# Row maxima of the first layer: one transfer per group into the query stack in place of four

## The chip, the cores and the metric

The kernel runs on one core of one Trainium2 chip. A core has five engines that work side by side, each on its own list of instructions in order: TensorE (PE: matmuls, with the loading of weights, PEld, counted apart), VectorE (DVE), ScalarE (ACT), GpSimd (POOL) and SyncE (SP). Transfers run on sixteen DMA engines; here SP and ACT issue them, and the issuing instruction stands in the queue of that engine. The metric is the device time in microseconds (us). Before the change the median of three runs is 1673.33 us (1674.31, 1663.47, 1673.33).

## What is computed

Two layers of cross attention, one after the other, over x of shape (16, 256, 320) with a context of shape (16, 256, 512); 20 heads of 16. In the first layer the first 77 context rows are text and the other 179 are image tokens:

```
logits   = q_h @ k_text.T * scale              ; probs = softmax(logits)         # per head
scores   = q_h @ k_ip.T  * scale
text_probs = softmax(q @ k_text.T * scale)      # all heads together
sem      = (text_probs @ text) @ ip.T * scale
ip_probs = softmax(scores + 0.5 * sem) * mask
out      = (probs @ v_text + ip_probs @ v_ip) @ Wout + bout + x
```

Each row of each head has two softmaxes, over text and over image tokens, so there are two maxima per row and head to be subtracted before the exponential. The second layer has 252 text rows and 4 image tokens, and is not touched by the change.

## The kernel before

**Tiling.** Everything is kept transposed where matmuls want it. A batch (of 16) has five *groups* of four heads, so each layer has 80 groups; the main loop has one *slot* per group (`slot0` for the first layer, `slot1` for the second), and beside the groups' work a list of tasks with due times fills the slots with projections, the semantic path, outputs and weights (`fill`). TensorE's order of work is as recorded (it is pinned); that of ACT, DVE, POOL and SP is put together when the program is built, by a scheduler that works through its own estimate of the times, within the dependencies and within a few orders that the code asks for (`queued`, `anchor`).

**A group of the first layer.** The *stacks* Q (`qs`) and K (`ks`) are tiles of 128 partitions by four heads by 256 columns, four of each in rotation. SP loads them (line 82, `stacks0`): 48 rows of query and key parts from DRAM (`qs<-qd`, `ks<-kd`), and 77 rows of the semantic path (`qs<-tph`, `ks<-M`). Rows 125 and 126 of K hold a constant indicator of text and image columns, loaded once (`ks<-mt`); rows 125 and 126 of Q are to hold the maxima: row 125 the maximum over text, row 126 that over image tokens, each for four heads and 256 queries.

The steps around the change, with the lines of the profile:

- `score0(k, t)`: four matmuls (L649) make the scores S of half t of group k. Two reductions on DVE take the maxima over the first 77 columns (L650) and over the other 179 (L651) into `mn`.
- `maxima0(k)`: two matmuls with the identity (L657) turn `mn` into eight rows of 256; ACT copies them to `mt` (L659; there is one such buffer); transfers (L661) bring them to rows 125 and 126 of Q, one per head, from the two rows of `mt` that belong to it. They are issued on ACT's queue, but for groups 0 and 1, whose maxima are issued on SP ahead of the loop (`begin`).
- `turned0(k, t)`: four matmuls (L673) of the whole stacks, 127 rows, make the scores with the maxima subtracted, transposed (T, two banks of PSUM); two exponentials on ACT (L676) make P, and POOL multiplies with the semantic factors (L679). For t = 1 the exponentials stay behind the last of the next group's issues (`queued(exp, issues[k + 1])`).
- `attend0(k)`: 24 matmuls of P with the values (L709), then `settle0` on DVE and POOL (L720 to L729).

Slot k holds, in this order, `maxima0(k + 1)`, `score0(k + 2, 0)`, `turned0(k, 0)`, other work, `attend0(k - 1)`, `score0(k + 2, 1)`, `turned0(k, 1)`, the loads of group k + 4, and other work. So a group's maxima leave about one slot before T needs them.

**Semaphores of transfers.** In the built program eight semaphores serve the transfers of both queues, handed out in turn in the scheduler's order; each issue also waits for the transfer eight before it, which had the same semaphore.

Of the kernel before, what the change touches and what calls it, by code (L numbers as in the profile page):

```python
# [9 lines left out]
FR = mybir.dt.float32r  # L10
AF = mybir.ActivationFunctionType
ALU = mybir.AluOpType
AX = mybir.AxisListType
# [10 lines left out]
T0 = 77  # L24
# [7 lines left out]
KS0 = 127  # L32
KS1 = 50
XROW = 48
# [14 lines left out]
def xattn2(  # L49
# [27 lines left out]
    nc = tc.nc  # L77
    f = lambda ap: ap.bitcast(F32)
    mm = nc.tensor.matmul
# [9 lines left out]
    def bank(tag="X"):  # L89
        return ps.tile([128, 512], F32, tag=tag, name=tag, bufs=BANKS[tag])  # L90

    def scores():

        return ps.tile([128, 1024], F32, tag="S", name="S", bufs=1).rearrange("p (h t) -> p h t", h=4)
# [4 lines left out]
    def buf(tag, shape, dtype=F32, bufs=1, name=None):  # L99
        if tag in ("wB", "wD", "vr", "raw"):  # L100
            return sb.tile(shape, dtype, tag=tag, name=name or tag, bufs=bufs)
        size = 1
        for d in shape[1:]:
            size *= d
        if tag not in slots:
            slots[tag] = [0, dtype] + [const_tile([128, max(size, words.get(tag, 0))], f"{tag}_{i}", dtype) for i in range(bufs)]
        n, kind, *ring = slots[tag]
        assert kind == dtype and len(ring) == bufs, tag
        slots[tag][0] += 1
        t = ring[n % bufs][: shape[0], :size]  # L110
        names = "abcd"[: len(shape) - 1]
        if len(names) > 1:
            t = t.rearrange(f"p ({' '.join(names)}) -> p {' '.join(names)}", **dict(zip(names, shape[1:])))
        return t

    def const_tile(shape, tag, dtype=F32):
        return const.tile(shape, dtype, tag=tag, name=tag)
# [7 lines left out]
    ident_r = const_tile([128, 128], "ident_r", FR)  # L125
# [15 lines left out]
    def anchor(inst):  # L141
        anchors[inst.ins.engine] = inst
        return inst
# [496 lines left out]
    maxes, issues = {}, {}  # L640

    def score0(k, t):
        Q, K = QK[k]
        if t == 0:
            maxes[k] = buf("mn", [128, 2, 4, 2], FR, bufs=2)
        mn = maxes[k]
        sp = scores()
        for h in range(4):
            mm(sp[:, h], Q[: XROW + T0, h, t * 128 : (t + 1) * 128], K[: XROW + T0, h], start=True, stop=True)  # L649
        nc.vector.tensor_reduce(mn[:, t, :, 0], sp[:, :, :T0], axis=AX.X, op=ALU.max)  # L650
        anchor(nc.vector.tensor_reduce(mn[:, t, :, 1], sp[:, :, T0:], axis=AX.X, op=ALU.max))  # L651

    def maxima0(k, queue=nc.scalar):
        Q, mn = QK[k][0], maxes[k]
        mp = bank()
        for t in range(2):
            mm(mp[:8, t * 128 : (t + 1) * 128], mn[:, t].rearrange("p h a -> p (h a)"), ident_r, start=True, stop=True)  # L657
        mt = buf("mt", [8, S], FR)
        nc.scalar.copy(mt, mp[:8, :S])  # L659
        for h in range(4):  # L660
            issues[k] = queue.dma_start(f(Q[XROW + T0 : KS0, h]), f(mt[2 * h : 2 * h + 2]))  # L661

    def turned0(k, t):

# [355 lines left out]
    for c in range(B // 2):  # L1020
        n, k = 10 * c, [("k0", c)] if c else []
# [34 lines left out]
    def ahead(k, t):  # L1056
        if k < NS:
            score0(k, t)
        else:
            both1(k - 2, t)  # L1060
# [5 lines left out]
    def begin():  # L1066
# [15 lines left out]
        stacks0(2)  # L1082
        parts(k0)
        score0(0, 0)
        parts(v1)
        score0(0, 1)
        get("m0t", 1)
        maxima0(0, nc.sync)
        parts(v1)
        get(*v1)  # L1090
# [3 lines left out]
        score0(1, 1)  # L1094
        parts(("s0", 1))
        maxima0(1, nc.sync)
        parts(("k0", 1))
        resid0.append(load(xT_d[0], "xc"))
# [97 lines left out]
```

## Time and profile before

| | us |
|---|---|
| runs | 1674.31, 1663.47, 1673.33; median 1673.33 |
| profiled execution, span from first to last instruction | 1663.4 |
| TensorE busy | 1533.5 (92%) |
| DVE busy | 1317.2 (79%) |
| POOL busy | 1202.2 (72%) |
| ACT busy (issuing not counted) | 877.7 (53%) |
| last issue of the first layer's maxima | 746.6 |
| granted TensorE clock, mean | 0.974 |

The page gives no time of the profiled execution but its span; the lowest of the runs is 0.07 us above it. A row of the profile names the engine, the line of the kernel, the operation and out<-in by the program's names. "Idle before <- X" says how long the engine stood idle and what ended that. The engine names with a q (ACTq, SPq) are the engines' queues: time in them is spent issuing or waiting, and is not counted as busy. The chain of waits follows back from the last instruction to what released it, step by step.

### The profile page before, as it was taken

What the parts mean: (1) busy time and instruction counts of PE and PEld (TensorE: products, weight loads), DVE (VectorE), ACT (ScalarE), POOL (GpSimd) and SP (SyncE); (2) the same over time, 40 slices, a digit from 0 to 9 for tenths busy, and PEclk for the clock granted to TensorE, in tenths of its full rate; (3) what the DMA queues carried; (4) which work ended last, traced back from release to release, by engine and by line L of the source; (5) the groups of instructions that cost most, each with busy time, mean ns of one, the idle gap of its engine ahead of it and who ended that gap; (6) DMA issues with size and microseconds to landing.
All of it is one profiled execution on the core that took longest, in us unless ns stands there. A gap on an engine that the chain in (4) does not pass through costs nothing.

```text
span 1663.4 us, 35253 instructions
## 1 busy us (share of the span) xinstructions
PE 1533.5 (92%) x12666; PEld 1222.9 (74%) x12666; DVE 1317.2 (79%) x2484; ACT 877.7 (53%) x1865; POOL 1202.2 (72%) x1194
## 2 busy tenths in 40 slices
PE   7789999999999898789999999999999999999996
PEld 6677888787888786677677777777777777777754
DVE  5367676777776677867889889889888998899885
ACT  5344444444444445435656555655565556556563
POOL 3458787878787767767778777867876777777784
PEclk9899999999999899899999999999999999999998
DMA  7867777777776676655424342434243324332301
GB/s 219 218 196 212 200 215 197 211 202 213 198 220 194 192 203 185 159 178 153 147 66 129 106 128 90 133 106 129 85 131 113 120 89 131 117 105 82 115 17 43
DMA packets 247739, 247.43 MB, mean 149 GB/s; under 512 B 31050, under 2 KB 231468, under 8 KB 247564
## 3 DMA queue, kind: packets, MB, share of 16 engines
q1 hardware_dynamic: 245356, 243.87, 49.7%
q8 instruction: 101, 1.65, 0.4%
q10 hardware_dynamic: 2208, 1.30, 0.3%
q14 instruction: 74, 0.61, 0.1%
HBM read 121.21 MB, written 88.18 MB: 126 GB/s over the span
## 4 chain that ended last, share of the span: by engine, by line
PE 55%; DVE 18%; DMA 10%; POOL 4%; SPq 4%; issue 3%; ACT 3%; ACTq 0%; DVEq 0%; POOLq 0%
PE X L205 14%; PE X L814 12%; PE X L522 8%; PE P L709 5%; DMA qs<-qd 4%; SPq L82 4%; PE S L649 3%; DVE mn L781 3%; DVE wt L818 3%; PE T L673 3%; PE P L826 3%; PE T L775 2%; DVE wt L816 2%; PE P L828 2%; DVE ho L512 2%
## 5 line engine op out<-in xcount | busy, mean ns | idle before, releaser
L679 POOL TENSOR_TENSOR P<-P,rs 128x512 f32<-128x512 f32 x320 | 412.2, 1309 | 169.3 <-ACT P L676 169.0
L805 POOL TENSOR_TENSOR wt<-P,ctb 128x512 f32<-128x512 f32 x320 | 451.0, 1424 | 76.0 <-ACT ctb L804 75.6
L814 PE MATMUL X<-ctb,gm 128*128 128x512 f32 x1120 | 329.3, 412 | 2.5 <-DVE wt L816 2.5
L676 ACT ACTIVATE P<-T 128x512 f32<-128x512 f32 x320 | 176.1, 595 | 233.8 <-PE T L673 128.3
L786 ACT ACTIVATE P<-T 128x512 f32<-128x512 f32 x320 | 173.9, 597 | 138.8 <-PE T L775 137.4
L816 DVE TENSOR_TENSOR wt<-X,wt 128x512 f32<-128x512 f32 x320 | 215.3, 678 | 17.4 <-PE X L814 16.9
L804 ACT ACTIVATE ctb<-P 128x512 fp32r<-128x512 f32 x320 | 195.3, 632 | 61.5 <-PE X L814 60.8
L814 PEld LDWEIGHTS X<-ctb,gm 128*128 128x128 f32 x1120 | 189.6, 188 | 48.6 <-DVE wt L816 5.2
L781 DVE TENSOR_REDUCE mn<-S 128x4 fp32r<-128x1008 f32 x160 | 191.1, 1194 | 0.6 <-PE S L780 0.6
L651 DVE TENSOR_REDUCE mn<-S 128x4 fp32r<-128x716 f32 x160 | 142.6, 891 | 0.0
L673 PE MATMUL T<-qs,ks 127*128 127x256 f32 x640 | 112.5, 296 | 22.9 <-DVE tmp L726 9.9
L709 PE MATMUL P<-P,vr 128*32 128x256 f32 x1920 | 129.3, 405 | 0.0
L649 PE MATMUL S<-ks,qs 125*128 125x256 f32 x640 | 117.7, 308 | 11.7 <-DMA ks<-kd 4.6
L649 PEld LDWEIGHTS S<-ks,qs 125*128 125x128 f32 x640 | 88.7, 195 | 48.6 <-issue 38.4
L522 PE MATMUL X<-ho,wF 128*128 128x256 f32 x768 | 112.4, 289 | 6.7 <-DVE ho L512 2.9
L522 PE MATMUL X<-hq,wE 128*128 128x256 f32 x768 | 111.9, 289 | 5.8 <-ACT hq L511 3.1
L818 POOL TENSOR_TENSOR wt<-wt 128x512 f32<-128x512 f32 x80 | 103.3, 1292 | 14.8 <-DVE wt L816 14.7
L673 PEld LDWEIGHTS T<-qs,ks 127*128 127x128 f32 x640 | 93.0, 198 | 28.0 <-DVE tmp L726 11.9
L522 PEld LDWEIGHTS X<-ho,wF 128*128 128x128 f32 x768 | 103.0, 194 | 12.5 <-DVE ho L512 4.6
L522 PEld LDWEIGHTS X<-hq,wE 128*128 128x128 f32 x768 | 102.7, 194 | 11.4 <-POOL hq L512 5.2
L650 DVE TENSOR_REDUCE mn<-S 128x4 fp32r<-128x308 f32 x160 | 74.9, 468 | 44.1 <-PE S L649 43.6
L818 DVE TENSOR_TENSOR wt<-wt 128x512 f32<-128x512 f32 x80 | 106.1, 1326 | 2.1
(201 smaller groups left out, 2973.9 us busy)
## 6 DMA issues: line engine op xcount, KB each, us to landing
qd<-q SPq DMA_DIRECT2D x96, 384.0 KB
qs<-tph SPq DMA_DIRECT2D x64, 308.0 KB
kd<-kst SPq DMA_DIRECT2D x73, 256.0 KB
rawc<-in_cT_dram SPq DMA_DIRECT2D x60, 256.0 KB
qs<-qd SPq DMA_DIRECT2D x80, 192.0 KB
ks<-kd SPq DMA_DIRECT2D x80, 192.0 KB
ks<-kd SPq DMA_DIRECT2D x160, 96.0 KB
qs<-qd SPq DMA_DIRECT2D x160, 96.0 KB
```

The source lines that it names most:

```text
L205: last = mm(out, lhs(a, k), rhs(b, k), start=i == 0, stop=i == len(terms) - 1)
L522: mm(pp, w(s, k, slice(m * 128, (m + 1) * 128)), a[:, t], start=i == 0, stop=i == len(terms) - 1)
L649: mm(sp[:, h], Q[: XROW + T0, h, t * 128 : (t + 1) * 128], K[: XROW + T0, h], start=True, stop=True)
L673: mm(st[p][:, j], K[:KS0, 2 * p + j, t * 128 : (t + 1) * 128], Q[:KS0, 2 * p + j], start=True, stop=True)
L679: anchor(nc.gpsimd.tensor_mul(pt, pt, rs[:, t : t + 1].to_broadcast([128, 2, S])))
L709: mm(pv[32 * s : 32 * s + 32, o : o + S], v[:, vt, h : h + 32], P[k, s // 2][:, t, s % 2], start=vt < 2, stop=vt != 1,)
L781: anchor(nc.vector.tensor_reduce(maxes[k + 2][:, t], sp[:, :, :T1], axis=AX.X, op=ALU.max))
L804: nc.scalar.activation(R[k, u][:, t], P[k, u][:, t], AF.Copy, scale=0.5)
L805: anchor(nc.gpsimd.tensor_sub(W[k, u][:, t], P[k, u][:, t], f(R[k, u][:, t])))
L814: mm(yp, gm[:, gb], R[k, u][:, kt], start=i == 0, stop=i == len(blocks[n]) - 1)
L816: nc.vector.tensor_mul(w[:, n], yp, w[:, n])
L818: (nc.vector if u else nc.gpsimd).tensor_add(w[:, 0], w[:, 0], w[:, 1])
```

## The change

`mn` is laid out by half, kind (text or image) and head instead of half, head and kind. So the turned rows of `mt` come as four text rows and then four image rows, which is the order of rows 125 and 126 of Q with four heads each, and one transfer of 8 KB takes the place of four of 2 KB. The reductions write their four results side by side instead of at every other place.

```diff
     def score0(k, t):
         Q, K = QK[k]
         if t == 0:
-            maxes[k] = buf("mn", [128, 2, 4, 2], FR, bufs=2)
+            maxes[k] = buf("mn", [128, 2, 2, 4], FR, bufs=2)
...
-        nc.vector.tensor_reduce(mn[:, t, :, 0], sp[:, :, :T0], axis=AX.X, op=ALU.max)
-        anchor(nc.vector.tensor_reduce(mn[:, t, :, 1], sp[:, :, T0:], axis=AX.X, op=ALU.max))
+        nc.vector.tensor_reduce(mn[:, t, 0], sp[:, :, :T0], axis=AX.X, op=ALU.max)
+        anchor(nc.vector.tensor_reduce(mn[:, t, 1], sp[:, :, T0:], axis=AX.X, op=ALU.max))

     def maxima0(k, queue=nc.scalar):
...
-            mm(mp[:8, t * 128 : (t + 1) * 128], mn[:, t].rearrange("p h a -> p (h a)"), ident_r, start=True, stop=True)
+            mm(mp[:8, t * 128 : (t + 1) * 128], mn[:, t].rearrange("p a h -> p (a h)"), ident_r, start=True, stop=True)
         mt = buf("mt", [8, S], FR)
         nc.scalar.copy(mt, mp[:8, :S])
-        for h in range(4):
-            issues[k] = queue.dma_start(f(Q[XROW + T0 : KS0, h]), f(mt[2 * h : 2 * h + 2]))
+        issues[k] = queue.dma_start(f(Q[XROW + T0 : KS0]), f(mt))
```

## The prediction

> **What bounds the kernel now.** I read the page first, then the busy time by stage, then who waited for whom on TensorE, then the stretch in which it waited longest for the transfers that change.
>
> The span, and the busy time by stage (columns: stretch in us, its length, busy us and instructions of PE, PEld, DVE, ACT and POOL, granted TensorE clock, DMA share, GB/s):
>
> ```profile
> span 1663.4 us, 35253 instructions
> ...
> 0.00:65.00 65.00, 45.52 (x270) 42.10 (x270) 30.10 (x74) 26.84 (x61) 18.95 (x28) 0.94 0.77 225
> 65.00:145.00 80.00, 72.47 (x630) 64.01 (x630) 52.15 (x115) 38.04 (x89) 55.45 (x50) 0.94 0.67 192
> 145.00:565.00 420.00, 394.45 (x3603) 337.94 (x3601) 297.52 (x673) 205.79 (x477) 324.79 (x304) 0.97 0.73 207
> 565.00:755.00 190.00, 163.38 (x1438) 134.45 (x1439) 141.47 (x301) 86.38 (x195) 131.34 (x124) 0.91 0.64 181
> 755.00:1663.40 908.40, 857.70 (x6730) 644.35 (x6729) 795.93 (x1324) 520.65 (x1045) 671.66 (x691) 0.99 0.34 106
> ```
>
> The changed lines work for the first layer only, which ends near 750. There TensorE bounds: 394.45 of 420 us in the steady stage, while ACT, whose issues the change removes, is busy for 205.79 (and issues for some 115 more: four of 0.57 us in each of 50 groups). A gain can come from three places alone: TensorE's idle time (25.55 us in the steady stage), its clock below 1.00, and the start. What ended TensorE's idle time from 65 to 565 (sum, times, longest, in us):
>
> ```profile
> PE X L571 <- DMA kb<-kd: 10.1, 2, 5.8
> PE T L673 <- DMA qs<-mt: 8.8, 10, 1.5
> PE S L649 <- DMA ks<-kd: 4.6, 4, 1.4
> ...
> PE S L649 <- DMA qs<-qd: 2.7, 3, 1.6
> ...
> PE X L657 <- ACT P L676: 0.6, 1, 0.6
> ```
>
> The second row is the transfer of the change: T (line 673) multiplies the query stack with the maxima rows in it. Those waits stand in five places, once per ten groups, 1.8 us each on average. One of them, on ACT's queue, on TensorE and in the chain of waits:
>
> ```profile
> 222.76 0.57 ACTq L661 DMA_DIRECT2D qs<-mt  x1
> ...
> 223.53 0.57 ACTq L661 DMA_DIRECT2D qs<-mt  x1
> ...
> 226.57 1.89 ACTq L661 DMA_DIRECT2D qs<-mt  x2
> ```
> ```profile
> 228.80 0.39 PE L673 MATMUL T<-qs,ks 127*128 127x256 f32 x1
> 229.85 0.39 PE L673 MATMUL T<-qs,ks 127*128 127x256 f32 x1 [0.66 <-DMA qs<-mt]
> 231.30 0.64 PE L673 MATMUL T<-qs,ks 127*128 127x256 f32 x2 [1.06 <-DMA qs<-mt]
> ```
> ```profile
> 179.42 2.70 DMA qs<-mt
> ...
> 222.63 4.97 DMA qs<-qd
> 227.62 3.54 DMA qs<-mt
> 231.30 0.64 PE T L673 x2
> ...
> 266.66 5.60 DMA qs<-qd
> ```
>
> The first two of the four issues go out at once; the third starts 3 us later, and the fourth at 227.62, just as the load of the stack's query rows (qs<-qd) lands. These rows don't overlap. The reason stands in the built program: the DMAs of both queues share eight semaphores, handed out in turn, and an issue waits until the DMA eight before it has landed. Third and fourth of this group follow such loads. So TensorE waits for an issue held on ACT by an unrelated transfer.
>
> It costs more than the idle time. The granted clock in the 8 us behind each of the five places (some 83 us apart), and between two of them:
>
> ```profile
> 147.80:155.80 8.00, 7.89 (x61) 6.03 (x61) 5.21 (x11) 3.62 (x10) 5.61 (x6) 0.79 0.86 218
> 231.30:239.30 8.00, 8.00 (x61) 6.88 (x62) 5.79 (x15) 3.65 (x11) 6.37 (x7) 0.79 0.92 247
> 313.60:321.60 8.00, 7.97 (x51) 6.10 (x52) 4.79 (x12) 3.23 (x10) 4.83 (x6) 0.59 0.91 230
> 397.80:405.80 8.00, 7.98 (x61) 6.48 (x61) 5.40 (x12) 3.63 (x11) 6.08 (x7) 0.79 0.92 243
> 480.40:488.40 8.00, 7.93 (x61) 6.84 (x61) 4.76 (x15) 3.62 (x10) 6.12 (x6) 0.79 0.84 213
> ...
> 239.30:311.30 72.00, 69.80 (x661) 60.48 (x659) 51.70 (x115) 35.17 (x80) 55.77 (x53) 1.00 0.71 200
> ```
>
> Behind every wait the clock falls to 0.79 or 0.59; between two waits it is 1.00.
>
> **The change, part by part.** *The issues.* What one costs its queue (minimum, median, maximum in ns):
>
> ```profile
> L661 ACTq DMA_DIRECT2D qs<-mt x312: 569/570/1203, 70.0 to 746.6; - x156
> ...
> L661 SPq DMA_DIRECT2D qs<-mt x8: 562/585/686, 51.2 to 64.1; - x8
> L82 SPq DMA_DIRECT2D ks<-mt x4: 622/752/915, 24.1 to 30.6; - x4
> ```
>
> Of 80 groups, 78 issue on ACT and two, before the loop, on SP. An issue with the new shape (8 KB into two partitions of four heads) isn't in the trace. From below it is bounded by 570 ns (the 2 KB one), from above by 915 ns; I take 752 ns, the median of ks<-mt, which also writes 2 x 4 x 256. ACT's queue gets back 4 x 570 - 752 = 1528 ns a group, 119 us in all. With both ends it is 106 to 133 us. By itself this buys nothing, since ACT still has some 100 us of the steady stage free.
>
> *The wait at every tenth group.* Ten groups hold 102 DMAs before and 72 after (30 fewer from ACT). Over some 83 us, eight DMAs last 6.5 us before and 9.2 us after; the loads that hold the issues take 4.97 to 5.60 us in the chain. In the built program the one issue of the stalled groups (9, 19, 29...) has a maxima transfer of the group before as its predecessor, long landed, so it goes out right after the copy, as the first of the four does today. Issued at 222.8 with 0.75 us, and with the 3.54 us that the late one took, it lands near 227.1, 1.7 us before the first T at 228.80. The row for this says 8.8 us of idle time: -8.8. The clock loss behind it goes too: 8 x (4 x 0.21 + 0.41) = 10.0 us.
>
> [...]
>
> How long the new transfer is in flight is the other unknown. It is bounded from below by the 2 KB flights (2.70 us is the shortest that I see in the chain, 3.54 here) and from above by a load of 192 KB, 4.97 us, which would land near 227.8 to 228.5: still ahead of T. [...]
>
> *The start.* SP's queue is occupied without a break here, and TensorE then waits for its load:
>
> ```profile
> 51.25 2.56 SPq L661 DMA_DIRECT2D qs<-mt  x4
> ...
> 59.70 2.30 SPq L82 DMA_DIRECT2D kb<-kd  x2
> 62.10 2.52 SPq L661 DMA_DIRECT2D qs<-mt  x4
> ```
> ```profile
> 65.28 2.85 PE L571 MATMUL X<-kb,q 128*128 128x192 f32 x12 [5.79 <-DMA kb<-kd]
> ```
>
> kb's load is issued 2.56 - 0.75 = 1.8 us earlier, and the context loads behind group 1 3.6 us earlier. At least 1.8 us, at most 3.6 come off the path: I take 2.8.
>
> *What else moves.* TensorE's order of work is the same in both built programs, and so are ACT, DVE and POOL from the first groups of the second layer on. In the first layer the issue on ACT now stands ahead of both exponentials of line 676, where three of four stood between or behind them; a held issue holds both, the POOL products behind them, and attention on TensorE in the next slot. DVE's order shifts by neighbours (maxima against the softmax of the semantic path), POOL's in one place per ten groups. I cost these at nothing: DVE is busy 297.52 and POOL 324.79 of 420, so either catches up. The reductions now write four results side by side instead of every other word:
>
> ```profile
> L651 DVE TENSOR_REDUCE mn<-S 128x4 fp32r<-128x716 f32 x160 | 142.6, 891 | 0.0
> ...
> L650 DVE TENSOR_REDUCE mn<-S 128x4 fp32r<-128x308 f32 x160 | 74.9, 468 | 44.1 <-PE S L649 43.6
> ```
>
> 408 more elements read cost 423 ns, 1.04 ns each; the four written can shift by some 4 ns either way, at most 1.3 us over 320 reductions on an engine with that much room: nothing. Transpose, copy and layout cost are unchanged in shape.
>
> From 565 to 755 TensorE waits for DVE, whose order there is reshuffled:
>
> ```profile
> PE T L673 <- DVE tmp L726: 9.9, 2, 5.9
> ```
>
> I have no row for the new order and take nothing; one wait more or less like the longest (5.9 us) is the bound on either side.
>
> *Sum.* -8.8 - 10.0 - 2.8 = -21.6 us against the span of 1663.4, which the lowest run exceeds by 0.07: 1641.8. The median of the runs, 1673.33, is 9.9 above that; I assume the changed kernel's runs lie alike, so 1673.33 - 21.6 = 1651.7, rounded to 1651. What is late next is TensorE itself.
>
> **The rivals.** *More goes.* SP's issues wait on the same eight semaphores; with 9.2 us for eight DMAs instead of 6.5 the stack loads leave earlier too, and the waits of S for ks<-kd and qs<-qd (4.6 + 2.7 = 7.3) go, with as much clock to each as at T (10.0 / 8.8): another 15.6 us. 1636. Against it: these waits follow loads that start only when TensorE frees the stack.
>
> *The dips stay.* Idle time of this size isn't what lowers the clock; a different cause in that phase does, such as the DMA share of 0.84 to 0.92. Then only 8.8 + 2.8 = 11.6 us go: 1662. For it: S also waits up to 1.6 us, with the clock at 1.00 around it (239.30:311.30). Against it: five of five.
>
> [...]
>
> *The hold moves ahead of the exponentials (slower).* In groups 10, 20, ... 70 the one issue follows, in turn of semaphores, a store of the queries (qd<-q) recorded only about half a group, some 4 us, before it. With a flight of 5 us and SP behind its plan, ACT stands with both exponentials behind it. How long such a hold gets is on record:
>
> ```profile
> ACT P L676 <- DMA qs<-mt: 9.3, 4, 5.0
> ```
> ```profile
> 427.80 3.03 ACTq L661 DMA_DIRECT2D qs<-mt  x2
> ```
>
> At 5.0 us of TensorE and 2 us of clock (10.0 / 5), seven turns cost 49 us, less the 21.6: +27, 1700. It decides from the point where holds reach TensorE with more than 21.6 / 7 = 3.1 us per turn. Against it: the second row is a hold of some 2 us with both exponentials behind it, in another group today, and TensorE's only wait for ACT there is the 0.6 us of the list above.
>
> That the change doesn't do what it says is excluded: 80 transfers stand in the built program where 320 stood.
>
> **How the numbers follow.** Forecast 0.50 (1651, own range 1642 to 1661: start 1.8 to 3.6, one wait of 5.9 in the tail, the spread of the runs); more goes 0.14 (1636); the dips stay 0.09 (1662); late anyway 0.15 (1670); the hold 0.12 (1700). The range from 1630 to 1674 leaves out the hold and the ends of the others. One per cent, about what can be told from no change here, is 16.7 us: below 1656.6 lie four fifths and more of the forecast and all of "more goes": 0.57. Slower by over 1% is the hold, 0.12; the rest, 0.31, lies within.
>
> **What would show it.** In the changed profile: maxima issues of 0.57 to 0.92 us, 78 on ACT; the waits of T for qs<-mt under 2 us in all from 65 to 565; the clock at 1.00 in five places where it was 0.59 or 0.79; the steady stage's PE idle time near 17 us; the second layer at 908 us as before. I am wrong if T still waits for qs<-mt, if waits of T or L657 for ACT appear at every tenth group, or if the first layer keeps its length with those waits gone.

## The result

The changed kernel takes 1656.9 us (median; 1650.59 to 1663.78) where the kernel before, on the same chip, takes 1671.02 (1663.47 to 1674.31): a ratio of 0.992, with a 95% interval of 0.9893 to 0.9947. The gain is some 14 us or 0.8%. The forecast was 1651, with 1630 to 1674 as its range. The direction and the range hold; the size is two thirds of the one forecast, and most of it stands in another place than forecast.

All lines of the kernel behind 660 have a number one lower than before: T is L672, the exponentials L675, POOL's product L678.

**The page and the stages after.** The profiled execution took 1657.31 us; its span, and the stages (columns as in the prediction: stretch, length, busy us and instructions of PE, PEld, DVE, ACT, POOL, clock, DMA share, GB/s):

```profile
span 1654.5 us, 34959 instructions
```
```profile
145.00:565.00 420.00, 394.08 (x3654) 341.10 (x3650) 294.61 (x675) 205.94 (x478) 325.89 (x306) 0.98 0.74 208
565.00:755.00 190.00, 165.24 (x1508) 137.42 (x1507) 150.23 (x313) 92.57 (x209) 141.58 (x136) 0.94 0.70 193
755.00:1654.50 899.50, 850.41 (x6648) 638.38 (x6640) 788.23 (x1315) 514.93 (x1030) 662.25 (x680) 0.99 0.34 105
```

In the steady stage TensorE is busy for 394.08 of 420 us; it was 394.45. Nothing was gained there, although the wait that the forecast was about is gone. What TensorE waited for from 65 to 565 (sum, times, longest):

```profile
PE S L649 <- DMA qs<-qd: 12.4, 5, 2.9
PE X L571 <- DMA kb<-kd: 8.7, 2, 4.8
PE X L590 <- DVE sp L586: 8.0, 5, 1.6
...
PE S L649 <- DMA ks<-kd: 2.1, 2, 1.3
```

T's wait for qs<-mt (8.8 us, ten times) has no row any more. In its place S waits for the load of the query rows, five times, 12.4 us where it was 2.7; and the semantic path comes late at L590, five times, 8.0 us.

The clock, in one of the five places of the prediction and then behind four of the five waits of S:

```profile
231.30:239.30 8.00, 6.42 (x60) 5.15 (x59) 6.13 (x18) 3.37 (x10) 8.00 (x8) 1.00 1.01 264
...
272.00:280.00 8.00, 7.28 (x48) 5.54 (x49) 3.53 (x11) 1.87 (x6) 2.50 (x2) 0.58 0.69 167
355.00:363.00 8.00, 6.00 (x48) 5.01 (x49) 4.13 (x15) 2.19 (x8) 4.43 (x5) 0.79 0.89 206
438.00:446.00 8.00, 5.83 (x40) 4.48 (x40) 2.80 (x10) 1.90 (x7) 3.95 (x4) 0.57 0.78 186
522.00:530.00 8.00, 7.07 (x55) 5.24 (x56) 4.98 (x12) 2.76 (x8) 3.54 (x5) 0.79 0.82 189
```

The old place is at 1.00, as forecast, and so is the stretch behind the first and longest wait of S, 2.9 us just ahead of 188 (1.00 over 188 to 196). But the dips are not gone: behind S they cost an estimated 8 x (0.42 + 0.21 + 0.43 + 0.21) = 10.2 us, as much as the 10.0 behind T before, reckoned in the same way.

**Why S waits longer.** SP's queue, after and then before (start, us in the queue):

```profile
258.15 3.39 SPq L82 DMA_DIRECT2D qd<-q  x3
262.05 1.89 SPq L82 DMA_DIRECT2D kb<-kd  x2
...
266.55 1.04 SPq L82 DMA_DIRECT2D qs<-qd  x1
```
```profile
259.02 1.93 SPq L82 DMA_DIRECT2D qd<-q  x2
262.90 1.05 SPq L82 DMA_DIRECT2D kb<-kd  x2
...
267.64 0.38 SPq L82 DMA_DIRECT2D qd<-q  x1
```

And the chain of waits after, where the load lands:

```profile
266.55 6.07 DMA qs<-qd
272.63 0.09 issue
272.72 1.19 PE S L649 x4
```

The prediction quotes the same load of before: issued at 266.66, 5.60 us in flight. The load lands at 272.26 before and at 272.62 after: here SP's queue and the flight set that time, not the maxima. The changed kernel's order also puts the third store of the queries ahead of the load where it went behind it. TensorE came to S sooner and waited there. This is followed up for one of the five places; the four others are taken to be like it.

**Where the gain is.** The copy of each group's maxima (mt<-X on ACT) marks the time of each group; the copies of the last group or two in two stretches, before and then after (count, durations in ns, first and last start):

```profile
L659 ACT CAST mt<-X x2: 356/356/357, 641.0 to 648.5; 8x256 fp32r<-8x256 f32 x2
L659 ACT CAST mt<-X x2: 341/351/361, 736.1 to 744.2; 8x256 fp32r<-8x256 f32 x2
```
```profile
L659 ACT CAST mt<-X x1: 360/360/360, 647.2 to 647.2; 8x256 fp32r<-8x256 f32 x1
L659 ACT CAST mt<-X x2: 342/352/362, 726.4 to 734.6; 8x256 fp32r<-8x256 f32 x2
```

Group 69 starts its copy at 648.5 and 647.2, group 79 at 744.2 and 734.6. From group 69 to 79 the stage takes 95.7 us before and 87.4 after. The two kernels are some 1.3 us apart at its beginning, 9.6 at its end, and 8.9 at the end of the span. So the profiled gain lies in the last ten groups of the first layer, where the second layer's weights, keys and queries are got ready. TensorE does the same matmuls there, some 640 in the trace, before and after:

```profile
648.50:744.20 95.70, 73.62 (x641) 58.59 (x640) 69.84 (x139) 38.30 (x85) 66.28 (x63) 0.88 0.64 181
```
```profile
647.20:734.60 87.40, 70.17 (x640) 55.30 (x640) 69.31 (x139) 37.95 (x85) 65.51 (x63) 0.92 0.72 197
```

Its idle time falls from 22.1 to 17.2 us, and its busy time by 3.4 us at a higher clock. ACT's queue and ACT itself, before and after, at group 76's issues:

```profile
714.97 4.49 ACTq L661 DMA_DIRECT2D qs<-mt  x3
719.56 1.09 ACT L676 ACTIVATE P<-T 128x512 f32<-128x512 f32 x2 [5.01 <-PE X L522]
```
```profile
711.69 0.65 ACTq L660 DMA_DIRECT2D qs<-mt  x1
712.45 2.07 ACT L675 ACTIVATE P<-T 128x512 f32<-128x512 f32 x4 [2.65 <-PE S L649]
```

Three issues of 0.57 us need 1.71 us; they took 4.49, so the queue was held for 2.8 us, and the exponentials stood behind it (the releaser named, X, was done before the last issue was: it is the issue). In the built program the transfers eight before these three are a stack load, a store of the second layer's keys and, ahead of the last, a load of x for the output, which SP sent late:

```profile
714.26 0.42 SPq L82 DMA_DIRECT2D xc<-in_xT_dram  x1
```

How much of the gain goes through this hold the profile doesn't settle. The chain of waits of before takes another way at this place: through a store of the second layer's keys, issued by SP, which POOL's queue waits for; only then come POOL's products, and T at 730.32 behind them:

```profile
715.82 5.41 DMA kd<-kst
...
721.95 2.80 POOL P L679 x2
```

The held exponentials end at 720.65, and the store lands at 721.23.

### The profile page after: what moved, and what is told of

Read it like the earlier page. It is cut to its first block, busy times and chain, and to the rows that moved or that the text cites. A ratio compares the mean times of both kernels' runs of the same rounds, so it can differ in the third digit from the quotient of the medians.

```text
span 1654.5 us, 34959 instructions
## 1 busy us (share of the span) xinstructions
PE 1526.7 (92%) x12666; PEld 1221.0 (74%) x12666; DVE 1313.8 (79%) x2484; ACT 877.5 (53%) x1865; POOL 1201.2 (73%) x1194
## 4 chain that ended last, share of the span: by engine, by line
PE 58%; DVE 19%; DMA 7%; POOL 5%; ACT 4%; issue 3%; SPq 1%; ACTq 0%; DVEq 0%; POOLq 0%
PE X L205 15%; PE X L813 12%; PE X L522 9%; PE P L708 5%; PE S L649 4%; DVE mn L780 3%; DVE wt L817 3%; PE T L672 3%; PE P L825 3%; PE T L774 2%; DVE ho L512 2%; DVE wt L815 2%; PE P L827 2%; POOL P L678 2%; DMA qs<-qd 2%
## 5 line engine op out<-in xcount | busy, mean ns | idle before, releaser
L678 POOL TENSOR_TENSOR P<-P,rs 128x512 f32<-128x512 f32 x320 | 411.7, 1310 | 162.2 <-ACT P L675 161.7
L675 ACT ACTIVATE P<-T 128x512 f32<-128x512 f32 x320 | 175.8, 595 | 215.0 <-PE T L672 169.4
L649 PE MATMUL S<-ks,qs 125*128 125x256 f32 x640 | 117.5, 307 | 22.1 <-DMA qs<-qd 12.7
L522 PE MATMUL X<-ho,wF 128*128 128x256 f32 x768 | 116.8, 297 | 9.7 <-ACT ho L511 5.1
L522 PEld LDWEIGHTS X<-ho,wF 128*128 128x128 f32 x768 | 107.2, 202 | 15.5 <-DVE ho L512 6.5
L817 POOL TENSOR_TENSOR wt<-wt 128x512 f32<-128x512 f32 x80 | 103.3, 1291 | 14.7 <-DVE wt L815 14.6
L672 PE MATMUL T<-qs,ks 127*128 127x256 f32 x640 | 106.9, 291 | 1.4 <-DVE sp L574 1.4
L205 PE MATMUL X<-cta,wA 128*128 128x252 f32 (+1 forms) x720 | 98.3, 282 | 6.6 <-ACT wA L147 5.5
```

The source lines that it names most:

```text
L205: last = mm(out, lhs(a, k), rhs(b, k), start=i == 0, stop=i == len(terms) - 1)
L522: mm(pp, w(s, k, slice(m * 128, (m + 1) * 128)), a[:, t], start=i == 0, stop=i == len(terms) - 1)
L675: exp = anchor(nc.scalar.activation(pt, st[p], AF.Exp, scale=SCALE))
L678: anchor(nc.gpsimd.tensor_mul(pt, pt, rs[:, t : t + 1].to_broadcast([128, 2, S])))
L817: (nc.vector if u else nc.gpsimd).tensor_add(w[:, 0], w[:, 0], w[:, 1])
```

## The experiments

All ratios are against the kernel before on the same chip. The stages are read off the maxima's copies of the profiled executions, as above, in us:

| kernel | group 2 to 59 | 59 to 69 | 69 to 79 | from 79 on |
|---|---|---|---|---|
| before | 484.7 | 94.2 | 95.7 | 919.2 |
| before, second profile | 484.1 | 93.3 | 96.3 | 920.2 |
| changed | 487.7 | 90.4 | 87.4 | 919.9 |
| new order, four transfers | 484.9 | 93.0 | 97.2 | 918.7 |
| two transfers | 493.3 | 97.3 | 85.5 | 919.2 |
| one up to group 63, then four | 488.7 | 90.9 | 93.9 | 921.9 |
| four up to group 63, then one | 487.1 | 95.0 | 88.4 | 918.0 |
| one, and three to nowhere | 485.0 | 94.3 | 97.3 | 920.7 |
| one, and three copies | 489.4 | 91.8 | 85.3 | 920.3 |
| query rows first | 487.5 | 89.3 | 84.5 | 919.4 |
| semantic keys on ACT | 481.2 | 92.9 | 84.9 | 917.7 |
| the same from batch 3 | 482.7 | 92.7 | 84.4 | 920.5 |
| both mends | 484.6 | 89.2 | 85.0 | 920.3 |
| one, issued by POOL | 549.7 | 96.5 | 95.0 | 918.7 |

**A second profile of before.**

> The kernel before once more, for a second profile. If the stages repeat, groups 9 to 59 take 415 us within 2 and groups 69 to 79 take 96 us within 2, and the difference of the end of the layer belongs to the kernels; if they move by more than 5 us, it belongs to the execution.

It took 1667.18 us. Group 69 to 79 takes 96.3 us, the same as 95.7. Groups 9 to 59 take 411.8 against 415.4, outside the 2 us expected, but groups 2 to 9 take 72.3 against 69.3, so that 2 to 59 is the same within 0.6 us. The end of the layer belongs to the kernels; a few us within the earlier stages belong to the execution.

**Where the gain is: one part of the groups at a time.**

```diff
-        issues[k] = queue.dma_start(f(Q[XROW + T0 : KS0]), f(mt))
+        if k < 64:      # the other kernel: k >= 64
+            issues[k] = queue.dma_start(f(Q[XROW + T0 : KS0]), f(mt))
+            return
+        for h in range(4):
+            issues[k] = queue.dma_start(f(Q[XROW + T0 : KS0, h]), f(mt[h : 8 : 4]))
```

> One transfer per group for groups 0 to 63, four (in the new layout) for 64 to 79; 192 transfers fewer, a multiple of eight, so that the turn of the semaphores at group 64 is that of the kernel before. Theory 'end of the layer' (the waits of T that went came back at S, and the gain stands in groups 70 to 79, where issues were held on ACT ahead of the exponentials): no wait of T for qs<-mt before group 64, S waiting some 12 us for qs<-qd, and 0 to -4 us against the kernel before. Theory 'steady stage' (the gain is the T waits and the clock behind them, as forecast): -10 to -14 us.

> The reverse: four transfers (in the new layout) for groups 0 to 63, one for 64 to 79. Theory 'end of the layer': T waits for qs<-mt every tenth group as before, and still -9 to -14 us against the kernel before, with groups 70 to 79 taking some 87 us in place of 96. Theory 'steady stage': 0 to -4 us.

One transfer up to group 63 gives 0.9964 (0.9944 to 0.9984), 1663.1 us against 1668.47, or -5.4 us; one from group 64 on gives 0.9936 (0.9919 to 0.9953), 1659.25 us or -9.2. Together that is 14.6, about the whole. So some two thirds of the gain is the end of the layer; the third before it is more than "end of the layer" allowed, though its interval (some 3 to 9 us) reaches into the 0 to 4 expected. Some 2 to 3 us of it stand in the row 59 to 69 of the table (90.9 against 94.2 and 93.3), where groups 60 to 63 lie. The rest I can't place: the profiled execution of that kernel (1667.32 us) lies above its median and shows no gain ahead of group 59. There S waits as in the changed kernel, 11.9 us for qs<-qd, and T doesn't wait. In the other kernel T waits as before, and the gain is there all the same:

```profile
PE T L676 <- DMA qs<-mt: 7.9, 9, 1.2
```

**The order of the maxima alone.**

```diff
+        for h in range(4):
+            issues[k] = queue.dma_start(f(Q[XROW + T0 : KS0, h]), f(mt[h : 8 : 4]))
```

> The new order of the maxima (by kind, then head) with four transfers of one head each, from rows h and 4+h. Both theories: within 4 us of the kernel before. A rival, that the reductions' contiguous writes or the order that the scheduler finds for them bring the gain: -10 to -14 us.

1.0003 (0.999 to 1.0016): the new order of the maxima and the schedule that comes with it give nothing.

**Half the dose.**

```diff
+        for n in range(2):
+            issues[k] = queue.dma_start(f(Q[XROW + T0 + n : XROW + T0 + n + 1]), f(mt[4 * n : 4 * n + 4]))
```

> Two transfers per group (one per kind, four heads each). Theory 'end of the layer': the hold of issues at groups 70 to 79 depends on how many issues stand ahead of the exponentials, so between half and all of the gain, -7 to -14 us. Theory 'steady stage': only waits of T that go count; with 82 DMAs per ten groups in place of 102 some of them stay, -4 to -10 us.

0.9976 (0.996 to 0.9993), -4 us: less than half of the gain in all. The end of the layer has all of it (85.5 us from 69 to 79), but 2 to 59 lost 8.6 us: S waits 15.2 us for qs<-qd there. The number of issues isn't a dose that acts evenly. It also shifts which transfer stands eight ahead of which; that this is why the earlier groups lost isn't shown.

**Issues without their data, and ACT's time without issues.**

```diff
         issues[k] = queue.dma_start(f(Q[XROW + T0 : KS0]), f(mt))
+        for h in range(3):                      # three transfers to nowhere
+            i = 6 * (k % 4) + 2 * h
+            issues[k] = queue.dma_start(scrap[i : i + 2], f(mt[2 * h : 2 * h + 2]))
...
+        for h in range(3 if k > 1 else 0):      # the other kernel: three copies
+            issues[k] = nc.scalar.copy(scrap, f(mt).unsqueeze(1).to_broadcast([8, 2, S]))
```

> The changed kernel with three more transfers of 2 KB behind the one, on ACT's queue, from the maxima into a tile that nobody reads: the data go as in the changed kernel, the number of issues on ACT and the turn of the semaphores are those of the kernel before. Theory 'held issues' (issues on ACT that wait for their semaphore hold the exponentials behind them): the gain of the end of the layer goes, groups 69 to 79 take 93 to 98 us, and the whole is within 4 us of the kernel before. Rival 'data in one piece' (T has its rows sooner, whatever stands behind them on ACT): -10 to -14 us, as the changed kernel.

> The changed kernel with three copies on ACT of the maxima into a tile that nobody reads, in place of the three extra transfers of the earlier run: ACT's time is taken (some 0.6 us each, as an issue), but no semaphore and no transfer. Theory 'held issues': the copies wait for nothing, so the gain stays, -9 to -15 us against the kernel before, groups 69 to 79 in 86 to 90 us. Rival 'ACT's time' (four issues of 0.57 us per group are what stood in the way): 0 to -4 us, groups 69 to 79 in 93 to 98 us.

With three transfers to nowhere the ratio is 1.0004 (0.9991 to 1.0016): all of the gain is gone, although T has its rows in one piece and doesn't wait for them. (The scheduler put one of the three ahead of the real one in places.) From 65 to 565 TensorE has a wait for the exponentials that neither before nor the changed kernel has on its list:

```profile
PE X L522 <- ACT P L679: 6.1, 5, 2.8
```

With three copies it is 0.996 (0.9939 to 0.9981), -7 us. The stretch from 650 to 735, in the order before, three to nowhere, changed, three copies:

```profile
650.00:735.00 85.00, 62.92 (x539) 48.98 (x538) 61.83 (x124) 33.29 (x73) 59.22 (x57) 0.86 0.68 193
```
```profile
650.00:735.00 85.00, 62.19 (x534) 48.61 (x534) 62.15 (x125) 33.48 (x72) 59.65 (x58) 0.83 0.69 192
```
```profile
650.00:735.00 85.00, 67.91 (x616) 53.33 (x609) 66.70 (x136) 36.94 (x82) 63.87 (x61) 0.92 0.72 196
```
```profile
650.00:735.00 85.00, 69.31 (x638) 55.57 (x637) 69.89 (x137) 54.76 (x115) 64.72 (x64) 0.92 0.73 203
```

Where ACT is busy for 54.76 us, with the copies, TensorE gets 69.31 us of work done in these 85; where it is busy for 33 and holds issues, 62 to 63. So at the end of the layer it is not ACT's time that the three transfers cost. That it is ACT's standing still behind them fits, but these two runs don't separate it from the other things that a transfer brings and a copy doesn't: its traffic, and its place in the turn of semaphores, for which SP's issues wait too (39.7 us for ks<-kd from 65 to 565 before, 1.7 after). TensorE's waits of 650 to 745, before and with the three transfers to nowhere:

```profile
PE T L673 <- DVE tmp L726: 4.0, 1, 4.0
PE X L590 <- DVE sp L586: 3.2, 1, 3.2
PE T L673 <- DVE P L724: 2.2, 1, 2.2
...
PE X L205 <- ACT q L530: 1.5, 1, 1.5
```
```profile
PE T L676 <- DVE tmp L729: 3.9, 1, 3.9
PE X L590 <- DVE sp L586: 3.5, 1, 3.5
...
PE T L676 <- DVE P L727: 2.5, 1, 2.5
```

The waits of T come back with the transfers, and neither the changed kernel nor the one with copies has any there. (They wait elsewhere: the changed kernel 8.4 us at L657 for the maxima, where before has 5.8.) The last row of before is the one that leads straight to group 76's hold: the copy of q stands on ACT behind the held exponentials. Elsewhere ACT's time may have a price: with the copies (609 ns each) the table shows 1.7 us more up to group 59 and 1.4 from 59 to 69. The medians are 1660.93 us and, in another comparison, 1656.9; but the two intervals overlap, so whether there is such a price is open.

**The wait of S: order of SP's loads, and one load less.**

```diff
-    def stacks0(k, parts="KQTM"):
+    def stacks0(k, parts="QKTM"):
+        first = None
+        behind = queued if k > 3 else lambda x, *y: x
...
-                dma(K[0:XROW], ...)
+                behind(dma(K[0:XROW], ...), first)      # and likewise the two others
...
-            dma(kt[:, :, s], kd[0][b // 2, r]...)
+            nc.scalar.dma_start(kt[:, :, s], kd[0][b // 2, r]...)      # the other kernel
```

> The changed kernel, with the load of the stack's query rows issued on SP ahead of the three other loads of its stack from group 4 on (it went last). Theory 'the loads took over' (S waits for the last of the stack loads, 12.4 us from 65 to 565, and the clock falls behind it): S's wait for qs<-qd falls under 4 us, the steady stage is 5 to 20 us shorter, and the whole -18 to -33 us against the kernel before. Rival 'TensorE's own work' (what T and S wait is only what is left over): S waits for another of the four loads in its place, and the whole stays at -10 to -16 us.

> The changed kernel, with the two loads of the semantic keys (kb) on ACT's queue in place of SP's: SP has 1.9 us more ahead of the stack loads of the late groups. Theory 'the loads took over': S's wait for qs<-qd falls by 1 to 1.9 us per place (5 to 10 us of 12.4), and the whole is -15 to -25 us against the kernel before, unless ACT holds the kb issues. Rival 'TensorE's own work': -10 to -16 us.

With the query rows first: 0.9897 (0.9872 to 0.9922), 1652.32 us against 1668.69. S waits as long as in the changed kernel, for the load that is now the last of the four:

```profile
PE S L651 <- DMA ks<-kd: 12.2, 5, 2.9
```

That was the rival's forecast: not the one load, but the last of the stack decides. With the semantic keys on ACT: 0.9885 (0.9864 to 0.9907), 1650.92 us, 18 less than before; the interval overlaps that of the changed kernel. SP has two issues less ahead of the stack, and S's wait for qs<-qd falls from 12.4 to 2.3 us. Its waits and the steady stage:

```profile
PE X L571 <- DMA kb<-kd: 10.8, 4, 8.7
...
PE S L649 <- DMA qs<-qd: 2.3, 3, 1.4
```
```profile
145.00:555.00 410.00, 392.33 (x3674) 338.51 (x3670) 299.86 (x681) 205.76 (x478) 326.05 (x306) 1.00 0.75 211
```

Groups 9 to 59 take 403.3 us in place of 414.7, at a clock of 1.00. That is 11.4 us in this execution, what was to be had of S's waits and the dips behind them. At the start it gives 5 us back (the one wait of 8.7 us for kb).

**The two mends refined and together.**

> As the run with the semantic keys' loads on ACT's queue, but from the fourth batch on only: the first batches keep them on SP. In the earlier run the start lost 5 us (a wait of 8.7 us for kb) and groups 9 to 59 took 403.3 us in place of 414.7. Theory 'the loads took over': the 403 to 405 us stay and the start is the changed kernel's again (73 us from group 2 to 9), -20 to -25 us against the kernel before. Rival (the 5 us at the start were only moved ahead from later groups): -16 to -19 us, as the earlier run.

> Both mends together: the semantic keys' loads on ACT from the fourth batch on, and the load of the query rows first of its stack on SP. Theory 'the loads took over': 3.6 us of waits of S are left from 65 to 565 with the keys' loads moved alone; up to those and as much clock again can go, -19 to -26 us against the kernel before. Rival ('the last of four loads decides, whichever it is', as the run with the query rows first has it: ks<-kd took the place of qs<-qd with 12.2 us): nothing further, -17 to -20 us.

From the fourth batch on: 0.9885 (0.9863 to 0.9906), no better than for all batches. The start has its 5 us back (73.3 us from group 2 to 9), but groups 9 to 59 take 409.4. So the sum is the rival's, but its reason, that the 5 us only move, isn't shown: S waits as little as in the run for all batches (1.5 us for qs<-qd, 2.1 for ks<-kd), and what is missing is clock, 0.98 where that run has 1.00:

```profile
145.00:555.00 410.00, 391.08 (x3607) 337.38 (x3607) 295.63 (x672) 202.36 (x471) 320.83 (x302) 0.98 0.75 210
```

A part of the 11.4 us therefore belongs to that one execution or to its clock. Both together: 0.9859 (0.9832 to 0.9886), 1648.27 us against 1670.49, or -22 us. This is the fastest kernel here; its interval lies below the changed kernel's.

**No issue on ACT.**

```diff
+        if k > 1:
+            nc.gpsimd.dma_start(f(Q[XROW + T0 : KS0]), f(mt))
+            return
```

> The changed kernel with the one transfer of each group issued by POOL from group 2 on, so that no issue of the first layer's maxima stands ahead of the exponentials. Theory 'held issues': TensorE's waits for the semantic path (X L590 for DVE, 8.0 us from 65 to 565, behind an issue held at every tenth group) fall under 4 us, and the whole is -14 to -20 us against the kernel before, if POOL's issue costs little. Rival 'POOL' (busy for 316 of 410 us in the steady stage; what an issue costs there no run shows): POOL's products come later and the whole is 0 to +30 us.

1.0409 (1.0387 to 1.0431): 1738.91 us, 68 by the ratio more than before, and more than twice what the rival had as its worst. L590's wait is gone from the list, but so is the pace (549.7 us from group 2 to 59), and POOL's issue itself is not dear (582 ns). The issues, TensorE's wait at T, and the durations of one form on DVE (minimum, median, maximum in ns), here and then in the changed kernel:

```profile
L661 POOL DMA_DIRECT2D qs<-mt x78: 582/582/706, 74.1 to 811.4; - x78
```
```profile
PE T L675 <- DVE mn L651: 31.4, 5, 6.4
```
```profile
L513 DVE SCALAR_TENSOR_TENSOR ho<-ho,tmask,hT x32: 469/1506/4958, 136.5 to 1721.9; 128x256 fp32r<-128x256 f32 x32
```
```profile
L513 DVE SCALAR_TENSOR_TENSOR ho<-ho,tmask,hT x32: 471/678/1521, 135.1 to 1644.9; 128x256 fp32r<-128x256 f32 x32
```

T now waits for the maxima of DVE; in the place looked at, they stand behind such an instruction of 5 us. So this run says little on the hold: that L590's wait went can have come from the slower pace. What the hold costs in the steady stage stays open.

## Why the prediction was right or wrong

- **T's waits, -8.8.** They went, all ten. But the sum took the idle time as gained, and it was not: "what is late next is TensorE itself" is the step that failed. The load of the query rows was late next, once per ten groups like T. It lands when SP's queue and its flight let it (272.26 and 272.62), so that what TensorE gains at T it waits at S: 12.4 us for 2.7. From group 2 to 59 the changed kernel took 487.7 us, and before 484.7 and 484.1. The prediction had that row, at 1.6 us, and read it only as something that might go too.
- **The clock, -10.0.** The price was right and the place was not. With T's waits gone the clock is 1.00 where it dipped, at a DMA share of 0.97 to 1.03, so "the dips stay" falls for these places; but 10.2 us of dips stand behind S. The clock also moves with the execution: from 65 to 145 it is 0.94 in the first profile of before and 0.89 in the second, while both have 0.98 from 145 to 555. That both could be had together is shown once, by the run with the semantic keys on ACT: 11.4 us less from group 9 to 59, clock 1.00. From the fourth batch on alone, the same change gave 5.3 us at 0.98.
- **The issue's cost.** 621 ns where 752 was taken (570 to 915 as bounds): an issue with two partitions of four heads costs 51 ns more than one of 2 KB, and ACT's queue got back 4 x 570 - 621 = 1659 ns a group, not 1528. On SP the two take 711 ns. Of ACT's time the prediction said that it buys nothing by itself. At the end of the layer that held (three copies cost nothing there); over the whole it is open.
- **The start, -2.8.** The wait for kb at 65 us fell from 5.79 to 3.90 us. What is left of it is not to be seen: group 9's copy starts at 138.93 and 143.67 in two executions of before and at 142.06 after.
- **The end of the layer, taken as nothing with 5.9 us either way.** This is the term that was mis-sized, and the one that made the result: 8.3 to 8.9 us from group 69 to 79, beyond the bound, and about 3 more from 59 to 69. The list of before had its waits, T for tmp with 9.9 us; the prediction put them down to DVE's order, had no row for the new one, and so took nothing. What the runs show is that the three transfers bring the loss there, and neither ACT's time nor the order of the maxima. The mechanism that fits is the one that the prediction saw at T (issues held by the transfer eight before), with the exponentials, not T, behind the held issue; the prediction weighed that only as a harm of the change. It is seen at group 76 and reaches TensorE at q, 1.5 us; whether the rest comes from it or from SP's issues, held in the same way, stays open.
- **More goes, 1636.** Wrong: S's waits rose from 7.3 to 14.5 us. Its premise came true: SP's waits for ks<-kd, ks<-M and qs<-tph fell from 39.7, 23.2 and 17.3 us to 1.7, 2.7 and 1.3 (65 to 565). But SP then waits for TensorE's T to free the stack, 89.1 us for 65.9: the reason that the prediction held against this rival was right.
- **The hold, 1700.** It occurs, small. The issue of group 20, with its copy done at 230.1, goes out when the store of the queries has landed, and one of the two exponentials stands behind it; in the chain of waits, then on ACT:

```profile
227.12 4.82 DMA qd<-q
...
232.01 0.62 ACTq L660
...
238.00 0.33 PE X L590
```

It reaches TensorE at L590 with 1.6 us per ten groups (8.0 us in five), about half of the 3.1 us from which it was to decide.

- **Late anyway, 1670** (the new transfer comes too late for T, and only the start is gained). From 65 to 565 no row of T waiting for the new transfer, where 8.8 us stood before: it falls.
- **The second layer** took 919.9 us from group 79's copy on, against 919.2 and 920.2: unchanged, as forecast.

The signs that the prediction named split. T's row went, the clock is 1.00 in the five places, 78 issues stand on ACT; but TensorE's idle time in the steady stage is 25.9 us and not 17, and "the first layer keeps its length with those waits gone" came true up to group 59. So that the time lies in the range is in part luck: 18.8 of the 21.6 us forecast stood on T's waits and their dips, which gave nothing in all, and a term that was taken as nothing gave some 12 us (both rows from group 59 to 79).

What moving an issue to another queue is worth is shown in part. The kb loads, moved from SP's queue (1.89 us for two) to ACT's, shorten S's waits for its load from 12.4 to 2.3 us. But what three transfers to nowhere cost here, the whole gain, is not the time to start them alone (570 ns each): three copies of 609 ns each don't take it at the end of the layer (85.3 us from group 69 to 79, against 97.3). The wait for a semaphore in the queues fits, though the transfers' own traffic isn't separated from it.

## What to carry to other kernels

A wait at the end of a list that recurs at the same step may stand in front of another of nearly the same depth (here 8.8 us at T, then 12.4 at S): before taking its idle time as gained, ask when the next operand lands and what sets that time. Where transfers of several queues share semaphores in turn, as in this program, a transfer can be a brake for everything behind it in its queue (at group 76 ACT's queue was held for 2.8 us); here fewer of them paid most at the change from one layer to the next, where SP has other loads and stores to send. And a trace with little in the steady stage needs its ends read as closely: this change gained more in the last ten groups than in all those before.

## What the runs showed of the hardware that was not expected

- The granted clock fell to 0.57 to 0.79 over 8 us behind waits of S of 2.1 to 2.8 us, as it did before behind T's shorter ones (0.59 to 0.79 behind 1.6 to 2.0 us in two waits); but behind the longest, 2.9 us at 188 in the changed kernel, it stayed at 1.00. So the length of one wait doesn't decide it alone; what does, no run here shows. With S's waits mostly gone its mean was 1.00 over 410 us in one run (semantic keys on ACT) and 0.98 in another (the same from batch 3 on).
- A transfer issued by POOL took 582 ns of POOL, where the same one took 621 ns of ACT's queue in the changed kernel; but with POOL issuing, the same DVE instruction of 128x256 (L513, ho) took up to 4.96 us, with a median of 1.51, where its longest was 1.52 in the changed kernel and its median 0.68. What stretched it, no run here shows.
